# Attention keys placed by 64 KB SBUF-to-SBUF transfers instead of through DRAM

## The chip, the cores and the metric

The kernel runs on one core of a Trainium2 chip. The metric is the device time of one execution in microseconds; a kernel is given by the median of several runs. The profile is that of one execution.

## The reference

The input is x, [2048, 128] in float32. Four layers each do half a feed-forward, a mixer, and half a feed-forward again, each on the layer norm of x and added to x:

```python
x = x + 0.5 * _L2_ffn_ref(_layernorm(x, axis=-1), L2_ffn_w_gate, L2_ffn_w_up, L2_ffn_w_down)
x = x + _L2_attn_ref(_layernorm(x, axis=-1), L2_attn_Wq, L2_attn_bq, ...)
x = x + 0.5 * _L2_ffn_ref(...)
x = x + 0.5 * _L3_ffn_ref(_layernorm(x, axis=-1), L3_ffn_q_w, ...)
x = x + _L3_attn_ref(_layernorm(x, axis=-1), L3_attn_Wq, ...)
x = x + 0.5 * _L3_ffn_ref(...)
```

Layer 0 has a low-rank feed-forward and a causal attention of one head, layer 1 a mixture of 8 experts and a long convolution. The change is in layers 2 and 3, which hold four attentions of 16 heads with 8 dimensions a head:

```python
# L2 and L3 attention: rotary q and k (L3 is causal)
q, k = rope(x @ Wq + bq), rope(x @ Wk + bk)
ctx = softmax(q @ k.T / sqrt(8)) @ v          # per head
out = ctx @ Wo + bo
# each L3 feed-forward: attention with scaled scores, a gate, then experts
scores = q @ k.T / sqrt(8) * 2 * sigmoid(q . scale_w)
attn = (out * sigmoid(out @ gate_w + gate_b)) @ out_w
x = ln(src + attn); y = ln(x + the higher-numbered of the two best experts of x)
```

## The kernel before

x stays in SBUF. Its 2048 rows are worked in NC = 4 chunks of CW = 512. The four attentions run in the order rope2 (layer 2), gated[0] (layer 3's first feed-forward), rope3 (layer 3, causal) and gated[1] (layer 3's second feed-forward). There are 16 chunks of keys in all.

**Where keys live.** One SBUF tensor `kp` [128, 8, 2048] holds the keys of all heads: heads 2p and 2p+1 lie at free index p, in rows 0 to 63 and 64 to 127 (j is 0 or 1). In a half of 64 rows, the first 32 are four groups of 8 dimensions: high part, low part, high part, low part of the key. The query tile `qp` has high, low, low, high, so a single product of TensorE in a fast format gives all four partial products. `round_hi` (L747) makes the high part `hi`, a subtraction makes `lo`; both are [128, 512] tiles with one row for each head and dimension.

**How keys get there.** `send` (L688) writes `hi` and `lo` to a DRAM tensor `dk` (L694, two writes of 256 KB). `load_keys` (L707, transfers at L713) then reads them back in a different shape, 16 rows of `kp` for 4 values of p at a time: 8 transfers of 128 KB for a chunk, all on SP. Queries go the same way through `dq`, and `begin` (L865) loads those of a unit (one chunk of queries, four heads) with two `qp<-dq` transfers (L871).

**Order of work.** `attend` (L856) runs an attention. Its steps are interleaved with other work, and a mode says what may lie beside them: "free" outside `attend`, "fill" until the first weights are there, "core", and "drain", when all its own scores are made and the next attention's chunks are already prepared. In free and fill `queue()` (L608) alternates between ScalarE's and SP's queue; otherwise it is SP. `value` and `query` of the attention, `prepare` (L720: norm, keys, and for chunk 0 the query) of the next one, and the feed-forwards are generators that are advanced beside the loop. In free mode the key loads of a chunk wait in `waiting_keys` until `attend` begins, and it issues them before `begin`. In drain the first half (p 0 to 3) is loaded at once, the other half at the start of the next `attend`.

In core and drain, the order of TensorE and VectorE instructions is that of the program. Elsewhere a scheduler of the framework sets it, by readiness. Each engine works its own list in order, so a transfer's issue on ScalarE or SP that must wait holds everything behind it. Each transfer issued from SP or ScalarE uses one of 8 completion semaphores in turn, shared by the two queues, so that the nth waits until the (n-8)th has landed.

The rotary chunks take their tables `cos` and `sin` from DRAM (L763), on SP in free mode and on GpSimd's queue otherwise; `project` (L771) multiplies them on VectorE into `rot`, adds on GpSimd (L784), rounds to `hi` on ScalarE, and subtracts to `lo` on GpSimd (in drain: all on VectorE). `hi`, `lo`, `cos`, `sin`, `rot`, `xc`, `hid` and others share one ring of 10 tiles.

Key stages, and how each chunk of keys is made:

| stage | keys of | chunks made in free or fill | chunks made in drain |
| --- | --- | --- | --- |
| T1, 676 to 860 us | rope2 | 4 | 0 |
| T2, 1521 to 1665 us | gated[0] | 2 | 2 |
| T3, 2480 to 2640 us | rope3 | 4 | 0 |
| T4, 3100 to 3215 us | gated[1] | 1 | 3 |

Of the kernel before, what the change touches and what calls it, by code (L numbers as in the profile page):

```python
# [11 lines left out]
F32 = mybir.dt.float32  # L12
# [11 lines left out]
D = 128  # L24
NT = S // P
CW = 512
NC = S // CW
TC = CW // P
E = 8
NH = 16  # L30
HD = 8
# [3 lines left out]
KD = 64  # L35
# [7 lines left out]
def tile_macaron(ctx: ExitStack, tc: tile.TileContext, a: dict, out: bass.AP):  # L43
    nc = tc.nc
# [4 lines left out]
    dram = ctx.enter_context(tc.tile_pool(name="dram", bufs=1, space=DRAM))  # L49
# [18 lines left out]
    order = {"pinned": False, "mode": "free"}  # L68
# [23 lines left out]
    def transpose(dst, src):  # L92
# [8 lines left out]
        out=anti, in_=anti, compare_op=ALU.not_equal, fill=1.0, base=-(P - 1),  # L101
# [5 lines left out]
        out=mask_qk, in_=mask_qk, compare_op=ALU.is_ge, fill=NEG, base=0,  # L107
# [5 lines left out]
        out=mask_kq, in_=mask_kq, compare_op=ALU.is_ge, fill=NEG, base=0,  # L113
# [14 lines left out]
        out=before, in_=before, compare_op=ALU.is_ge, fill=1.0, base=0,  # L128
# [24 lines left out]
    for c in range(NC):  # L153
        loads[c % 2].dma_start(
            out=x[:, c * TC : (c + 1) * TC, :],
            in_=a["x"][c * CW : (c + 1) * CW, :].rearrange("(t p) d -> p t d", p=P),
# [451 lines left out]
    def queue():  # L608
        turn["q"] += 1
        return nc.scalar if order["mode"] in ("free", "fill") and turn["q"] % 2 else nc.sync  # L610
# [57 lines left out]
    class Heads:  # L668
# [19 lines left out]
        def send(self, which, c):  # L688
            hi, lo = ring("hi"), ring("lo")
            yield from self.project(which, c, hi.bitcast(F32R), lo.bitcast(F32R))  # L690
            parts = (hi, lo, lo, hi) if which == "q" else (hi, lo)
            d = (dq if which == "q" else dk)[c]
            for n, part in enumerate(parts):
                queue().dma_start(out=d[:, n * HD : (n + 1) * HD, :], in_=part)  # L694
            if which == "q":
                self.sent.add(c)
            elif self.current:
                self.load_keys(c)
            elif order["mode"] == "drain":
                self.load_keys(c, (0,))  # L700
                self.waiting_keys.append((c, (1,)))
            else:
                self.waiting_keys.append((c, (0, 1)))
            yield 1


        def load_keys(self, c, halves=(0, 1)):  # L707
            for h in halves:
                ps = slice(4 * h, 4 * h + 4)
                for j in range(2):  # L710
                    for n in range(2):
                        r = j * KD + n * 2 * HD
                        nc.sync.dma_start(  # L713
                            out=kp[r : r + 2 * HD, ps, c * CW : (c + 1) * CW].bitcast(F32),
                            in_=rows_of(dk[c], j)[:, ps, :],
                        )
            if 0 in halves:
                self.loaded.add(c)

        def prepare(self, c):  # L720
            yield from self.normed(c)
# [27 lines left out]
    def rows_of(d, j):  # L749
        return d.rearrange("(p j) r w -> j r p w", j=2)[j]  # L750

    class RopeHeads(Heads):
# [3 lines left out]
            self.v_weight = wp[pre + "_v"]  # L756
            self.xnT = {}

        def tables(self, c):
            for name in ("cos", "sin"):  # L760
                t = ring(name)
                where = nc.sync if order["mode"] == "free" else nc.gpsimd
                where.dma_start(out=t, in_=a[f"{self.pre}_{name}"][:, c * CW : (c + 1) * CW])  # L763
                yield t

        def normed(self, c):
# [2 lines left out]
            yield from normed_chunk(c, xn, self.xnT[c])  # L769

        def project(self, which, c, hi, lo):  # L771
            tables = list(self.tables(c))
            cols = self.wp[self.pre + "_bcol"]
            n = 0 if which == "q" else 2
            ps = banks("pj")
            for k, half in enumerate("AB"):
                mm(ps[:, k, :], self.wp[f"{self.pre}_{which}{half}"], self.xnT[c])
            turned = [ring("rot") for _ in range(2)]
            for k in range(2):
                vec.scalar_tensor_tensor(  # L780
                    turned[k], ps[:, k, :], cols[:, n + k : n + k + 1], tables[k], ALU.add, ALU.mult
                )
            engine = vec if order["mode"] == "drain" else nc.gpsimd
            engine.tensor_tensor(turned[0], turned[0], turned[1], ALU.add)  # L784
            round_hi(hi, turned[0])
            engine.tensor_tensor(lo, turned[0], hi.bitcast(F32), ALU.subtract)
            yield 1
# [68 lines left out]
    def attend(A, carried, follow, after=None):  # L856
# [1 line left out]
        KR = 4 * HD  # L858
        HV = HD + 1
        A.current = True  # L860
        for c, halves in A.waiting_keys:
            A.load_keys(c, halves)
        units, queries, weights = A.units, A.queries, A.weights

        def begin(B, u):  # L865
# [139 lines left out]
        n = nw = 0  # L1005
        while nw < len(weights) or last:
# [5 lines left out]
            if w and (ready.get(w[0], n + 1) > n or w[1] // TC not in A.valued):  # L1012
                w = None
# [380 lines left out]
    og = dram.tile([(E + XT) * P, D], F32, name="og")  # L1394

    rest = dram.tile([KD, CW], F32, name="rest")
    dk = [dram.tile([NH, 2 * HD, CW], F32, name=f"dk{c}") for c in range(NC)]
    dq = [dram.tile([NH, 4 * HD + 2, CW], F32, name=f"dq{c}") for c in range(NC)]
    def zero_tables():
        with tc.tile_pool(name="zero2", bufs=1) as tmp:  # L1400
# [80 lines left out]
def _rope_tables(ang):  # L1481
    half = HD // 2
    cos = np.empty((NH, HD, S), np.float32)
    sin = np.empty((NH, HD, S), np.float32)
    cos[:, :half], cos[:, half:] = np.cos(ang).T, np.cos(ang).T
    sin[:, :half], sin[:, half:] = -np.sin(ang).T, np.sin(ang).T
    return cos.reshape(D, S), sin.reshape(D, S)


def _layout(i):  # L1490
    f = np.float32
    half = HD // 2
# [12 lines left out]

    r = {
        "x": i["L0_attn_input_data"].reshape(S, D),
        "qk": i["L0_attn_qk"], "ov": i["L0_attn_ov"],
        "l0_WT": i["L0_ffn_W"].T, "l0_VT": i["L0_ffn_V_r"].T, "l0_CT": i["L0_ffn_C"].T,
        "l0_b": i["L0_ffn_b"],  # L1510
        "shift": shift,
        "aT": i["L1_attn_a"].reshape(NP, P).T,
        "bT": i["L1_attn_b"].reshape(NP, P).T,
        "cT": i["L1_attn_c"].reshape(NP, P).T,
        "l1_gT": i["L1_ffn_gate_w"].T,
        "l1_w12T": i["L1_ffn_w12"].transpose(2, 0, 1),
        "l1_w3T": i["L1_ffn_w3"].reshape(E, D, 2, P).transpose(3, 0, 2, 1),
        "l2_wgT": i["L2_ffn_w_gate"].T, "l2_wuT": i["L2_ffn_w_up"].T,
        "l2_wdT": i["L2_ffn_w_down"].reshape(D, 3, P).transpose(2, 1, 0),
    }  # L1520
    r["l2_cos"], r["l2_sin"] = _rope_tables(pos * inv2)
    r["l3_cos"], r["l3_sin"] = _rope_tables(pos * inv3)
    for pre, nm, t, oa, ob in (
        ("l2", "L2_attn", False, same, swap), ("l3", "L3_attn", True, odd_a, odd_b),
    ):
        w = {n: (i[f"{nm}_W{n}"].T if t else i[f"{nm}_W{n}"]) for n in "qkvo"}
        for n in "qk":
            r[f"{pre}_{n}A"], r[f"{pre}_{n}B"] = _ordered(w[n], oa), _ordered(w[n], ob)
        r[f"{pre}_bcol"] = np.stack(
            [_ordered(i[f"{nm}_b{n}"], o) for n in "qk" for o in (oa, ob)], axis=1,  # L1530
        )
        for n in "vo":
            r[f"{pre}_{n}"] = w[n]
            r[f"{pre}_b{n}"] = i[f"{nm}_b{n}"]

    sw = np.zeros((NH, HD, NH, HD), f)
    for h in range(NH):
        sw[h, :, h, :] = i["L3_ffn_scale_w"][h][:, None]
    r |= {
        "b3_q": i["L3_ffn_q_w"], "b3_k": i["L3_ffn_k_w"], "b3_sw": sw.reshape(D, D),  # L1540
        "b3_v": i["L3_ffn_v_w"], "b3_o": i["L3_ffn_out_w"], "b3_g": i["L3_ffn_gate_w"],
        "b3_gb": i["L3_ffn_gate_b"].reshape(D, 1),
        "b3_n1g": i["L3_ffn_n1_g"], "b3_n1b": i["L3_ffn_n1_b"],
        "b3_n2g": i["L3_ffn_n2_g"], "b3_n2b": i["L3_ffn_n2_b"],
        "b3_rs": i["L3_ffn_res_scale"],
        "b3_mg": i["L3_ffn_moe_gate_w"], "b3_mgb": i["L3_ffn_moe_gate_b"],
        "b3_b1": i["L3_ffn_b1"], "b3_b2": i["L3_ffn_b2"],
        "b3_wt": np.concatenate([
            i["L3_ffn_w1"],
            i["L3_ffn_w2"].reshape(E, 2, P, D).transpose(0, 2, 1, 3).reshape(E, P, 2 * D),  # L1550
            i["L3_ffn_ln_g"].reshape(E, 2, P).transpose(0, 2, 1),
            i["L3_ffn_ln_b"].reshape(E, 2, P).transpose(0, 2, 1),
        ], axis=2).reshape(E * P, WTN),
    }
    return {n: np.ascontiguousarray(v) for n, v in r.items()}
# [17 lines left out]
```

## Time and profile before

| what | value |
| --- | --- |
| median of 3 runs | 4069.42 us (4062.28 to 4075.64) |
| profiled execution | 4074.4 us, span 4072.6 us |
| TensorE busy | 3557.4 us (87%) |
| VectorE busy | 3141.5 us (77%) |
| ScalarE busy | 2329.1 us (57%) |
| GpSimd busy | 215.0 us (5%) |
| DMA | 111.91 MB, mean 27 GB/s |
| key loads `kp<-dk` | 128 of 128 KB |
| key writes `dk<-hi`, `dk<-lo` | 16 and 16 of 256 KB |

Times in the profile are microseconds from the start of the span. PE is TensorE, PEld its weight loads, DVE VectorE, ACT ScalarE, POOL GpSimd, SP the engine that issues most transfers; a q behind an engine's name (SPq, ACTq) means its issue of transfers. A group of instructions is written as "out<-in", with the line of the kernel. The number behind a bar, or in brackets, is the idle time of the engine just before the instruction, and "<-" names what ended it. The row of digits for the clock gives, for 40 equal slices, the TensorE clock that was granted, in tenths of full speed; the DMA row gives how busy the 16 DMA engines were.

### The profile page before, as it was taken

The numbers are of one execution on the slowest core, as the hardware profiler recorded it, in microseconds if no ns is written. First come the engines' busy times: TensorE is split into PE (matmuls) and PEld (weight loads), VectorE is DVE, ScalarE is ACT, GpSimd is POOL, SyncE is SP. The second block draws the span as 40 slices with busy tenths as digits, with TensorE's granted clock in tenths as the row PEclk, the third lists the DMA queues.
The fourth block names the chain that finished last, engine by engine and source line by source line (L and its number), as shares of the span: only waits on it lengthen the run. The fifth ranks groups of instructions, "written<-read, shape, count | busy, mean of one in ns | idle before, by whom it ended". The sixth has DMA issues, their size and how long they took to land. (4 is left out here: it accounts for less than half of the span.)

```text
span 4072.6 us, 72035 instructions
## 1 busy us (share of the span) xinstructions
PE 3557.4 (87%) x29080; PEld 1680.4 (41%) x29080; DVE 3141.5 (77%) x5645; ACT 2329.1 (57%) x4436; POOL 215.0 (5%) x262
## 2 busy tenths in 40 slices
PE   8789898689999995899999965599997899999965
PEld 8566664333333342333333343243333333333334
DVE  3855443579999975899999745689997799999844
ACT  1222122158888862688888722246675488888732
POOL 2000000100000000000000033100000000000013
PEclk8889798779999997899999966668998799999966
DMA  2100003220000002100000022400002200000012
GB/s 71 25 1 1 1 1 87 62 63 7 10 7 10 4 13 57 50 9 9 7 10 4 9 70 77 110 20 10 10 2 62 54 10 7 10 7 7 7 42 74
DMA packets 71532, 111.91 MB, mean 27 GB/s; under 512 B 9712, under 2 KB 29920, under 8 KB 70944
## 3 DMA queue, kind: packets, MB, share of 16 engines
q1 hardware_dynamic: 57536, 77.81, 7.2%
q0 software_dynamic: 7088, 20.81, 2.1%
q10 hardware_dynamic: 6576, 8.69, 0.8%
q8 instruction: 229, 3.75, 0.4%
q14 instruction: 103, 0.84, 0.1%
HBM read 74.47 MB, written 31.75 MB: 26 GB/s over the span
## 5 line engine op out<-in xcount | busy, mean ns | idle before, releaser
L83 DVE TENSOR_REDUCE h_mx<-sn 128x2 f32<-128x1024 f32 (+1 forms) x1856 | 2206.3, 1197 | 141.4 <-PE sn L886 119.8
L942 ACT ACTIVATE pr<-st 128x512 f32<-128x512 f32 x3712 | 1972.7, 585 | 518.7 <-PE st L75 335.7
L75 PE MATMUL av<-pr,va 128*32 128x256 f32 x14592 | 1191.4, 399 | 10.9 <-ACT h_ot L971 10.9
L75 PE MATMUL st<-qp,kp 64*128 64x512 f32 x3712 | 998.4, 500 | 49.2 <-ACT pr L942 45.6
L886 PE MATMUL sn<-kp,qp 64*128 64x512 f32 (+3 forms) x3712 | 812.1, 416 | 126.6 <-DMA qp<-dq 46.1
L75 PEld LDWEIGHTS st<-qp,kp 64*128 64x128 f32 x3712 | 394.4, 188 | 818.1 <-ACT pr L942 441.8
L75 PEld LDWEIGHTS av<-pr,va 128*32 128x32 f32 x14592 | 293.1, 109 | 664.7 <-issue 626.8
L886 PEld LDWEIGHTS sn<-kp,qp 64*128 64x128 f32 x3712 | 388.7, 195 | 186.6 <-issue 99.8
L75 PE MATMUL h<-xnT,w_l_w12T 128*128 128x512 f32 x512 | 250.1, 611 | 1.7 <-DVE xnT L65 1.7
L554 ACT ACTIVATE hid<-h 128x512 f32<-128x512 f32 x128 | 76.4, 597 | 301.4 <-PE h L75 301.4
L75 PEld LDWEIGHTS po<-w_l_w3T,hid 128*128 128x128 f32 x1024 | 131.2, 193 | 69.1 <-DVE hid L555 47.2
L563 DVE SCALAR_TENSOR_TENSOR x<-po,gate,x 128x128 f32<-128x128 f32 x256 | 71.9, 344 | 100.4 <-PE po L75 100.3
L75 PE MATMUL po<-w_l_w3T,hid 128*128 128x128 f32 x1024 | 139.9, 279 | 1.3 <-DVE hid L555 1.3
L555 DVE TENSOR_TENSOR hid<-hid,h 128x512 f32<-128x512 f32 x128 | 87.2, 683 | 55.1 <-PE h L75 55.1
L75 PEld LDWEIGHTS h<-xnT,w_l_w12T 128*128 128x128 f32 x512 | 90.2, 197 | 66.1 <-issue 62.6
L1270 POOL DMA_INDIRECT wt<-in_b_wt,w_row_i x30 | 28.8, 960 | 1436.6 <-DVE slot_i L83 1395.0
L915 ACT CAST h_mT<-mt_ps 8x512 fp32r<-8x512 f32 x64 | 36.9, 576 | 100.4 <-PE mt_ps L93 100.2
L83 DVE BATCH_NORM_STATS2 st<-ph 128x6 f32<-128x256 f32 x46 | 19.9, 432 | 87.0 <-PE ph L75 87.0
L223 POOL TENSOR_TENSOR x<-x,w_b_n2b 128x512 f32<-128x512 f32 x8 | 10.1, 1266 | 1301.1 <-DVE rows L83 1133.7
L93 PE MATMUL xn_tp<-ident,xn_t 128*128 128x128 f32 x64 | 20.1, 406 | 66.3 <-ACT xn_t L189 62.7
L83 DVE TENSOR_TENSOR sn<-sn,mask_qk 128x256 f32<-128x256 f32 x128 | 54.2, 426 | 30.7 <-PE sn L886 29.3
L83 DVE TENSOR_TENSOR st<-st,mask_kq 128x128 f32<-128x128 f32 x256 | 63.3, 291 | 14.0 <-PE st L75 13.4
(391 smaller groups left out, 2627.5 us busy)
## 6 DMA issues: line engine op xcount, KB each, us to landing
qp<-dq SPq DMA_DIRECT2D x128, 136.0 KB
kp<-dk SPq DMA_DIRECT2D x128, 128.0 KB
dq<-hi SPq DMA_DIRECT2D x23, 256.0 KB
dq<-lo SPq DMA_DIRECT2D x23, 256.0 KB
wt<-in_b_wt SPq DMA_DIRECT2D x16, 258.0 KB
kp<-rest SPq DMA_DIRECT2D x8, 512.0 KB
dk<-lo SPq DMA_DIRECT2D x16, 256.0 KB
qp<-h_mT SPq DMA_DIRECT2D x256, 4.0 KB
```

What stands on the lines that cost most here:

```text
L75: pin(nc.tensor.matmul(dst, lhsT=lhsT, rhs=rhs, start=start, stop=stop))
L83: ins = method(*args, **kw)
L93: pin(nc.tensor.transpose(dst, src, ident))
L223: nc.gpsimd.tensor_tensor(xs, xs, row.unsqueeze(1).to_broadcast([P, TC, D]), ALU.add)
L554: nc.scalar.activation(hid[:, hb, :], p_1, AF.Silu)
L555: nc.vector.tensor_tensor(hid[:, hb, :], hid[:, hb, :], p_2, ALU.mult)
L563: nc.vector.scalar_tensor_tensor(x[:, i, :], po[:, t, :], gate[:, i, e : e + 1], x[:, i, :], ALU.mult, ALU.add)
L886: pin(nc.tensor.matmul(sc[:, j, :wd], lhsT=qp[r, p, t * P : (t + 1) * P], rhs=kp[r, 2 * g + p, kc * CW : kc * CW + wd], start=True, stop=True,
L915: nc.scalar.copy(mT, pt)
L942: nc.scalar.activation(pr[:, off:CW], sc[:, off:], AF.Exp, scale=A.scale)
L1270: nc.gpsimd.indirect_dma_start(wts[k], None, a["b3_wt"], bass.IndirectOffsetOnAxis(ap=w_row_i[:, s - E : s - E + 1], axis=0),)
```

## The change

Keys made outside the drain go straight from `hi` and `lo` to `kp`, in 16 transfers of 64 KB a chunk: each takes 32 rows of `hi` or `lo` and fills 8 rows of `kp` for 4 values of p. They are issued from `queue()`, as soon as the chunk is made. In the drain, the first half goes this way (8 transfers on SP), the second is written to a smaller `dk` (two writes of 128 KB) and read back at the start of the next `attend` (8 transfers of 64 KB on SP).

For 32 neighbouring rows of `hi` to fill 8 rows for 4 values of p, the columns of the key weights, the key biases and the key tables are reordered when inputs are laid out (`by_rows`); for this, tables are now two sets, one for q and one for k, so the loads of the tables are as many as before. The issue order on SP also changes: without deferred loads, nothing of the keys stands at the start of `attend` except the second halves from the drain.

```diff
             if which == "q":
+                for n, part in enumerate(parts):
+                    queue().dma_start(out=dq[c][:, n * HD : (n + 1) * HD, :], in_=part)
                 self.sent.add(c)
-            elif self.current:
-                self.load_keys(c)
-            elif order["mode"] == "drain":
-                self.load_keys(c, (0,))
-                self.waiting_keys.append((c, (1,)))
+                yield 1
+                return
+            self.place_keys(c, 0, parts)
+            self.loaded.add(c)
+            if self.current or order["mode"] != "drain":
+                self.place_keys(c, 1, parts)
             else:
-                self.waiting_keys.append((c, (0, 1)))
+                for n, part in enumerate(parts):
+                    nc.sync.dma_start(out=dk[c][n], in_=part[KD:, :])
+                self.waiting_keys.append(c)
...
+        def place_keys(self, c, half, parts):
+            for n in range(4):
                 for j in range(2):
-                    for n in range(2):
-                        r = j * KD + n * 2 * HD
-                        nc.sync.dma_start(
-                            out=kp[r : r + 2 * HD, ps, c * CW : (c + 1) * CW].bitcast(F32),
-                            in_=rows_of(dk[c], j)[:, ps, :],
-                        )
+                    r, q = j * KD + n * HD, half * KD + j * 4 * HD
+                    queue().dma_start(
+                        out=kp[r : r + HD, 4 * half : 4 * half + 4, c * CW : (c + 1) * CW].bitcast(F32),
+                        in_=parts[n % 2][q : q + 4 * HD, :],
+                    )
+
+        def load_keys(self, c):
+            for n in range(4):
+                for j in range(2):
+                    r = j * KD + n * HD
+                    nc.sync.dma_start(
+                        out=kp[r : r + HD, 4:8, c * CW : (c + 1) * CW].bitcast(F32),
+                        in_=dk[c][n % 2].rearrange("(j d p) w -> j d p w", j=2, d=HD)[j],
+                    )
...
+    by_rows = np.arange(D).reshape(2, 4, 2, HD).transpose(0, 2, 3, 1).reshape(D)
...
+        for n in ("kA", "kB"):
+            r[f"{pre}_{n}"] = r[f"{pre}_{n}"][:, by_rows]
+        r[f"{pre}_bcol"][:, 2:4] = r[f"{pre}_bcol"][by_rows, 2:4]
...
-        "b3_q": i["L3_ffn_q_w"], "b3_k": i["L3_ffn_k_w"], "b3_sw": sw.reshape(D, D),
+        "b3_q": i["L3_ffn_q_w"], "b3_k": i["L3_ffn_k_w"][:, by_rows], "b3_sw": sw.reshape(D, D),
```

More of the change, by code (lines that the diff above doesn't have):

```diff
@@ L691, in send @@
             parts = (hi, lo, lo, hi) if which == "q" else (hi, lo)
-            d = (dq if which == "q" else dk)[c]
-            for n, part in enumerate(parts):
-                queue().dma_start(out=d[:, n * HD : (n + 1) * HD, :], in_=part)
             if which == "q":
+                for n, part in enumerate(parts):
+                    queue().dma_start(out=dq[c][:, n * HD : (n + 1) * HD, :], in_=part)
                 self.sent.add(c)
-            elif self.current:
-                self.load_keys(c)
-            elif order["mode"] == "drain":
-                self.load_keys(c, (0,))
-                self.waiting_keys.append((c, (1,)))
-            else:
-                self.waiting_keys.append((c, (0, 1)))
+                yield 1
@@ L704, in send @@
+                return
[3 more added lines that the diff above has]
+                self.place_keys(c, 1, parts)
+            else:
+                for n, part in enumerate(parts):
+                    nc.sync.dma_start(out=dk[c][n], in_=part[KD:, :])
+                self.waiting_keys.append(c)
             yield 1
-        def load_keys(self, c, halves=(0, 1)):
-            for h in halves:
-                ps = slice(4 * h, 4 * h + 4)
+        def place_keys(self, c, half, parts):
+            for n in range(4):
@@ L710, in load_keys @@
                 for j in range(2):
-                    for n in range(2):
-                        r = j * KD + n * 2 * HD
-                        nc.sync.dma_start(
-                            out=kp[r : r + 2 * HD, ps, c * CW : (c + 1) * CW].bitcast(F32),
-                            in_=rows_of(dk[c], j)[:, ps, :],
-                        )
-            if 0 in halves:
-                self.loaded.add(c)
+                    r, q = j * KD + n * HD, half * KD + j * 4 * HD
[3 more added lines that the diff above has]
+                    )
@@ L757, in __init__, with tables @@
             self.xnT = {}
-        def tables(self, c):
+        def tables(self, which, c):
             for name in ("cos", "sin"):
@@ L762, in tables @@
                 where = nc.sync if order["mode"] == "free" else nc.gpsimd
-                where.dma_start(out=t, in_=a[f"{self.pre}_{name}"][:, c * CW : (c + 1) * CW])
+                where.dma_start(out=t, in_=a[f"{self.pre}_{name}_{which}"][:, c * CW : (c + 1) * CW])
                 yield t
@@ L771, in project @@
         def project(self, which, c, hi, lo):
-            tables = list(self.tables(c))
+            tables = list(self.tables(which, c))
             cols = self.wp[self.pre + "_bcol"]
@@ L860, in attend @@
         A.current = True
-        for c, halves in A.waiting_keys:
-            A.load_keys(c, halves)
+        for c in A.waiting_keys:
+            A.load_keys(c)
         units, queries, weights = A.units, A.queries, A.weights
@@ L1396, in tile_macaron @@
     rest = dram.tile([KD, CW], F32, name="rest")
-    dk = [dram.tile([NH, 2 * HD, CW], F32, name=f"dk{c}") for c in range(NC)]
+    dk = [dram.tile([2, KD, CW], F32, name=f"dk{c}") for c in range(NC)]
     dq = [dram.tile([NH, 4 * HD + 2, CW], F32, name=f"dq{c}") for c in range(NC)]
@@ L1520, in _layout @@
     }
-    r["l2_cos"], r["l2_sin"] = _rope_tables(pos * inv2)
-    r["l3_cos"], r["l3_sin"] = _rope_tables(pos * inv3)
+    by_rows = np.arange(D).reshape(2, 4, 2, HD).transpose(0, 2, 3, 1).reshape(D)
+    for pre, inv in (("l2", inv2), ("l3", inv3)):
+        for n, t in zip(("cos", "sin"), _rope_tables(pos * inv)):
+            r[f"{pre}_{n}_q"], r[f"{pre}_{n}_k"] = t, t[by_rows]
     for pre, nm, t, oa, ob in (
```

## The prediction

> **What bounds the kernel now.** I read the page's totals first, then its slices, the costliest groups, the two DMA groups of the keys, and then the timeline of the four stretches in which keys are made.
>
> ```profile
> span 4072.6 us, 72035 instructions
> PE 3557.4 (87%) x29080; PEld 1680.4 (41%) x29080; DVE 3141.5 (77%) x5645; ACT 2329.1 (57%) x4436; POOL 215.0 (5%) x262
> PEclk8889798779999997899999966668998799999966
> DMA  2100003220000002100000022400002200000012
> L886 PE MATMUL sn<-kp,qp 64*128 64x512 f32 (+3 forms) x3712 | 812.1, 416 | 126.6 <-DMA qp<-dq 46.1
> kp<-dk SPq DMA_DIRECT2D x128, 128.0 KB
> ```
>
> TensorE is busy for 87%: inside an attention it sets the time, with VectorE close behind. No transfer of keys can matter there. It matters where the DMA row rises: these are the stages where keys are made, and the clock row dips at them (7 to 8, 6 in the third). Of the 126.6 us that TensorE was idle before `sn`, queries from DRAM ended 46.1. The busy time by stage:
>
> ```profile
> 676.00:860.00 184.00, 111.09 (x338) 53.55 (x336) 93.44 (x233) 30.73 (x61) 29.47 (x28) 0.69 0.41 103
> 860.00:1521.00 661.00, 653.29 (x6131) 253.76 (x6128) 622.93 (x679) 553.39 (x1027) 2.56 (x2) 0.99 0.02 7
> 1521.00:1665.00 144.00, 87.81 (x400) 41.81 (x398) 76.80 (x160) 35.64 (x68) 3.79 (x3) 0.75 0.28 67
> 2480.00:2640.00 160.00, 67.66 (x275) 33.62 (x276) 94.48 (x319) 34.29 (x78) 42.61 (x42) 0.63 0.39 102
> 3100.00:3215.00 115.00, 84.82 (x478) 38.27 (x477) 67.25 (x123) 44.15 (x87) 5.05 (x4) 0.74 0.37 86
> ```
>
> Columns: length, then busy time of TensorE, its weight loads, VectorE, ScalarE and GpSimd, the clock, DMA share, GB/s. In the four key stages T1 to T4 (603 us in all) no engine is full (TensorE 42 to 74%); the second row is an attention, where TensorE works 99%. So the end is set by a serial chain in T1 to T4: norm, projection, rotation, rounding, transfer, score. What queues on SP and ScalarE in these 603 us decides.
>
> **What the change removes and adds.** Before, each of 16 chunks of keys costs 2 writes of 256 KB and 8 loads of 128 KB: 10 transfers, 160 in all, the loads all on SP. After, the 11 chunks made outside the drain have 16 transfers of 64 KB (8 on ScalarE's queue, 8 on SP's); the 5 made in the drain (two in T2, three in T4) have 8, 2 writes of 128 KB, and 8 later loads, all on SP: 11 x 16 + 5 x 18 = 266. Compute is the same; tables for q and k are as many loads as before. What goes away is the DRAM round trip; what comes is 106 issues, and 8 x 11 = 88 key issues on ScalarE where `dk<-hi` was 11.
>
> **Price of one 64 KB transfer.** The trace has no such transfer, so I bound it. Issue: SBUF to SBUF exists in `qp<-h_mT`, four issues in 2.56 us, 0.64 us each. Eight on a queue are at least 8 x 0.64 = 5.1 us: the fast end. Flow:
>
> ```profile
> 1057.43 2.56 SPq L918 DMA_DIRECT2D qp<-h_mT  x4
> 670.00:690.00 20.00, 13.57 (x43) 7.24 (x42) 7.85 (x46) 5.46 (x12) 1.27 (x1) 0.76 1.07 206
> 819.00:824.00 5.00, 1.75 (x4) 0.78 (x4) 0.20 (x1) 0.00 (x0) 0.00 (x0) 0.50 1.07 155
> 1064.00:1068.00 4.00, 3.76 (x36) 1.64 (x32) 3.64 (x5) 3.12 (x7) 0.00 (x0) 1.00 0.15 55
> ```
>
> `kp<-rest` into 32 rows moves 206 GB/s, `kp<-dk` into 16 rows 155, and `qp<-dq` into 34 rows only 55, on 2 of 16 engines. [...] Each transfer also waits for the eighth before it on the two queues (8 completion semaphores in turn), which ties the queue that issues to landings.
>
> **T1, keys of rope2.**
>
> ```profile
> 697.40 0.60 SPq L694 DMA_DIRECT2D dk<-lo  x1
> 701.55 0.75 DVE L83 SCALAR_TENSOR_TENSOR rot<-pj,w_l_bcol,sin 128x512 f32<-128x512 f32 x1 [5.99 <-DMA sin<-in_l_sin]
> 729.50 0.53 ACTq L694 DMA_DIRECT2D dk<-hi  x1
> 731.39 0.60 ACT L646 ACTIVATE hid<-gu 128x512 f32<-128x512 f32 x1 [1.91 <-PE gu L75]
> 821.19 0.76 PE L886 MATMUL sn<-kp,qp 64*128 64x512 f32 x1 [12.88 <-DMA kp<-dk]
> ```
>
> Chunk 0: the q tables now stand on SP behind 8 key issues. VectorE already waits for `sin` (5.99 us), and behind it queue `xc` and the next chunk. Issues from 697.4 last 7 to 8 us, so 701.55 becomes about 708.5: +7 (fast +5, slow +16). Chunk 1: ScalarE issues its 8 from 729.5 until about 736.5 instead of 730.0; `hid`, due at 731.4, waits behind: +5 (fast +4, slow +11). Chunk 2 delays the `xc` copy in the same way, most of it covered by `hid`'s own chain: +1 (0.5 to 6). Chunk 3 is the direct path: lo is ready at 812.9, `sn` at 821.19, 8.3 us for write, receipt and first load, then 1 to 2 us more before 823.01. The new path needs about 6.5 for all pieces of half 0: -2 (fast -4, slow +2). Sum +11 (fast +5.5, slow +35).
>
> **T2, keys of gated[0].** In the drain SP alone carries 2 x 8 transfers and 4 writes ahead of q's four writes, so `qp<-dq`, which released `sn` at 1549.86, is about 3.5 later (0 to 8). Chunk 2 holds ScalarE ahead of `hid`: +1.5 (0 to 7.5). Chunk 3, with `sn` at 1642.24 after 4.63 us for `kp<-dk`: 0 (-2 to +6). Sum +5 (-1 to +21).
>
> **T3, keys of rope3: the gain.**
>
> ```profile
> 2551.80 0.53 SPq L694 DMA_DIRECT2D dk<-lo  x1
> 2552.37 15.29 SPq L713 DMA_DIRECT2D kp<-dk  x19
> 2568.21 11.34 SPq L871 DMA_DIRECT2D qp<-dq  x8
> 2573.51 0.44 PE L886 MATMUL sn<-kp,qp 64*128 64x128 f32 x1 [28.16 <-DMA qp<-dq]
> ```
>
> All key loads of three chunks are put off to the start of the attention and stand on SP ahead of the first query: TensorE idles 28.16 us. After, the keys are placed as they are made, and `qp<-dq` follows q's writes. Were nothing else late, `sn` could come about 21 us sooner. Against it: q's tables behind chunk 0's keys (+7), ScalarE's issues ahead of `xn_t` in chunks 0 and 1 (+3 to 4 each, one covered), and VectorE and TensorE work of the last experts that lay inside the idle 28 us must now be done after the first unit, some 5; the fourth chunk, made in the fill, holds ScalarE for +4. That is -21 + 7 + 4 + 5 + 4 = -1; since part of this lies in the same idle time (two holds at once count once), I take -4 (fast -14, slow +15).
>
> **T4, keys of gated[1].** As T2 with three drain chunks, but its chain has `sn` twice waiting for `qp<-dq` (11.29 and 1.88 us): +2 for the queue ahead of dq, +1 for 8-row loads of half 1, 0 for chunk 3: +3 (-2 to +17).
>
> **Sum.** 11 + 5 - 4 + 3 = +15 us. The profiled execution took 4074.4 with a span of 4072.6, so 4089.4 for such an execution. The runs of before have the median 4069.42 (4062.28 to 4075.64), 5.0 below the profiled one, so I put the +15 on the median: **4084 us**. All fast ends: 5.5 - 1 - 14 - 2 = -11.5; all slow ends: 35 + 21 + 15 + 17 = +88. Outside T1 to T4 I count nothing: TensorE covers it there (99% in the second row of stages). Were that cover gone, the 88 issues on ScalarE would cost 88 x 0.64 = 56 us; the part in T1 to T4 is priced above.
>
> **Rivals.** (A) The forecast. (B) Faster, by T3: if a chunk's transfers land in 5.1 us, the issue bound, the holds shrink to T1 +5.5, T2 0, T3 -16, T4 -1: -11.5 us, and -20 if the experts' work still fits into what idle time is left: 4050 to 4058. For it: 28.16 us of idle that only a queue's order causes, and 206 GB/s seen on one queue. Against: q's tables still stand behind 8 issues. It decides from about 5.5 us a chunk. (C) Costs and gain cancel: T3 gives -14 while T1, T2, T4 keep +14 to +19: 4068 to 4077. [...]
>
> **Chances.** About 0.3% (12 us) is what a measurement of this kernel can tell from no change. A 0.50, B 0.20, C 0.17, D 0.13. A's own range is 4072 to 4105, of which about a fifth lies within 0.3%. So faster 0.19 (B, nearly all beyond 4057), same 0.28 (C 0.17, a fifth of A, the edge of B), slower 0.53. The range for 8 in 10: leaving out the far end of D and of B, 4052 to 4122.
>
> **What would show it.** Right: in the page `kp<-hi` and `kp<-lo` on ScalarE's and SP's queues, 64 KB each; in T1 `rot` with `sin` near 708 and `hid` near 736, idle before them; in T3 the first `sn` well before 2573 with idle below 28.16; all of it within the key stages, the attentions unchanged in length. [...] Wrong: if the time moves inside the attentions, or the clock of T1 to T4 moves the sum.

## The result, and the profile after

The changed kernel takes 4115.93 us (median of 4 runs, 4104.34 to 4121.84), the kernel before on the same chip 4065.85 us (4051.9 to 4075.64). The ratio is 1.0122, with a 95% interval from 1.0083 to 1.0161: the change costs some 50 us. The forecast was 4084 us, with a range from 4052 to 4122.

The page of the changed kernel, the lines that answer to those of before:

```profile
span 4110.6 us, 72218 instructions
PE 3551.4 (86%) x29080; PEld 1671.1 (41%) x29080; DVE 3140.8 (76%) x5645; ACT 2327.7 (57%) x4436; POOL 215.1 (5%) x262
PEclk8999798679999997899999965578987799999966
L893 PE MATMUL sn<-kp,qp 64*128 64x512 f32 (+3 forms) x3712 | 811.1, 415 | 125.7 <-DVE h_mx L83 45.7
kp<-hi SPq DMA_DIRECT2D x64, 64.0 KB
```

Busy times are the same to 0.6%, so nothing is computed slower: TensorE waits longer. The 64 KB transfers are there (64 of each part on SP, 44 on ScalarE), and in the four slices around T3 (24th to 27th) the clock is 6, 5, 5, 7 where it was 6, 6, 6, 6. TensorE's idle time before `sn` is unchanged in sum (125.7 for 126.6), but `qp<-dq` no longer leads it. To see where the time went, I took the same instruction in both traces as a mark at each end of a key stage: T1 from the first cast `hi` of rope2 to its first `h_ot`; T2 from the 15th to the 17th `h_ot`; T3 from the first key projection of rope3 to the 41st `h_ot`; T4 from the 44th to the 49th `h_ot`. Before, these are 203.2, 226.6, 325.7 and 317.8 us (they are wider than the windows of the prediction). After:

| stage | forecast | measured |
| --- | --- | --- |
| T1 | +11 | +27.3 |
| T2 | +5 | +7.8 |
| T3 | -4 | +1.5 |
| T4 | +3 | +10.6 |
| sum | +15 | +47.2 |

Between the stages, the differences are under 1 us. The profiled spans differ by 38.0 and not 47.2 since this execution was 4.0 shorter ahead of T1 and 5.8 shorter behind T4, in work that the change doesn't touch.

T3's +1.5 is made of two parts of different kinds. Up to the first `h_ot` of rope3 it is 11.0 longer than before (119.0 for 108.0). From there to the end of T3 it is 9.4 shorter, and there the same 1346 products of TensorE take less time because the granted clock is 0.83 for 0.77. The two windows, before and after (columns as in the prediction; the clock is third from last):

```profile
2621.50:2839.10 217.60, 194.20 (x1346) 85.95 (x1346) 190.49 (x366) 113.37 (x246) 6.08 (x6) 0.77 0.08 25
2663.90:2872.10 208.20, 183.82 (x1346) 82.61 (x1346) 188.88 (x365) 112.66 (x246) 6.08 (x6) 0.83 0.08 26
```

So the placement of the keys lost 11 us in T3, and the clocks of these two executions hide 9.4 of it. (e7 below, which places keys as before, has the same 208.3 us and 0.83 in this part as the changed kernel.)

T1 and T3 in the changed kernel, from its timeline (VectorE and ScalarE in T1; TensorE and ScalarE in T3):

```profile
708.36 0.75 DVE L83 SCALAR_TENSOR_TENSOR rot<-pj,w_l_bcol,cos 128x512 f32<-128x512 f32 x1 [18.36 <-DMA cos<-in_l_cos_q]
749.75 1.08 ACT L646 ACTIVATE hid<-gu 128x512 f32<-128x512 f32 x2 [12.93 <-DMA kp<-hi]
2588.01 0.33 PE L893 MATMUL sn<-kp,qp 64*128 64x128 f32 x1
2597.28 1.26 ACT L189 ACTIVATE rows<-rows,ln_nb,ln_r 128x128 f32<-128x128 f32 x3 [12.44 <-DMA kp<-hi]
2612.09 1.02 PE L93 MATMUL mt_ps<-ident,h_mt 128*8 128x128 f32 x4
2624.24 1.65 ACT L189 ACTIVATE xn_t<-x,ln_nb,ln_r 128x128 f32<-128x128 f32 x4 [10.62 <-DMA kp<-hi]
2625.80 0.56 ACT L922 CAST h_mT<-mt_ps 8x512 fp32r<-8x512 f32 x1
2646.72 1.25 ACT L949 ACTIVATE pr<-st 128x384 f32<-128x384 f32 x3 [9.12 <-DMA kp<-hi]
```

VectorE stands 18.36 us for the q tables (before, 0.77 for `cos` and 5.99 for `sin`). ScalarE stands 12.93 us behind its own key issues before it can start `hid`. In T3 the first score comes without the 28.16 us of idle; counted from the start of the stage it is 17 us sooner. But between the scores and the exponentials (`pr`) stands a cast on ScalarE, `h_mT`, which the second product needs. Its input `mt_ps` is ready at 2613.1, and ScalarE comes to it at 2625.8, behind the issues of the third chunk's keys. Before, the first `h_mT` came 15.6 us after the first score; now it is 37.8. So the first exponential is 4.6 late. After the first four exponentials the issues of the fourth chunk take another 9.12 us, and the fifth is 10.8 late.

### The profile page after: what moved, and what is told of

Read it like the earlier page. It is cut to its first block, busy times and chain, and to the rows that moved or that the text cites. A ratio compares the mean times of both kernels' runs of the same rounds, so it can differ in the third digit from the quotient of the medians.

```text
span 4110.6 us, 72218 instructions
## 1 busy us (share of the span) xinstructions
PE 3551.4 (86%) x29080; PEld 1671.1 (41%) x29080; DVE 3140.8 (76%) x5645; ACT 2327.7 (57%) x4436; POOL 215.1 (5%) x262
## 5 line engine op out<-in xcount | busy, mean ns | idle before, releaser
L893 PE MATMUL sn<-kp,qp 64*128 64x512 f32 (+3 forms) x3712 | 811.1, 415 | 125.7 <-DVE h_mx L83 45.7
L75 PEld LDWEIGHTS po<-w_l_w3T,hid 128*128 128x128 f32 x1024 | 130.9, 192 | 68.8 <-DVE hid L555 47.2
L75 PE MATMUL gu<-xc,l_wgT 128*128 128x512 f32 x48 | 36.5, 852 | 45.7 <-DVE xc L65 23.5
```

Of the source, the lines that this page charges most:

```text
L75: pin(nc.tensor.matmul(dst, lhsT=lhsT, rhs=rhs, start=start, stop=stop))
L893: pin(nc.tensor.matmul(sc[:, j, :wd], lhsT=qp[r, p, t * P : (t + 1) * P], rhs=kp[r, 2 * g + p, kc * CW : kc * CW + wd], start=True, stop=True,
```

## The experiments

All stages are read as above, against the kernel before. Stages with the same code differed by 1.2 us in T1 (e8 and e9), 2.7 in T4 (e1, e9 and e11), 6 in T2 (e7 and before) and 8 in T3 (e4 and changed), so a stage's number from one profile is good to that. In T3 the 8 us lie behind its first `h_ot`: that last part took from 201.3 us (e4) to 217.7 (before), and over all kernels it is the longer the lower its clock, from 0.89 (e4) to 0.77 (before). The profile of before is the longest, so each T3 below is too low by 3 to 16 us. The column "T3, first" ends at the first `h_ot` and is nearly free of this; there changed and e4 differ by 1.2. Medians and ratios are of all runs, and they vary with the clock too: among the 31 runs of before beside e11, a mean clock lower by 0.001 goes with 2.3 us more (a line fitted to them).

| kernel | T1 | T2 | T3 | T3, first | T4 | sum of T1 to T4 | ratio to before (95%) |
| --- | --- | --- | --- | --- | --- | --- | --- |
| changed | +27.3 | +7.8 | +1.5 | +11.0 | +10.6 | +47.2 | 1.0122 (1.0083 to 1.0161) |
| e1 rows four apart | +10.8 | -1.0 | -8.9 | -5.4 | +5.7 | +6.6 | 1.0006 (0.9990 to 1.0022) |
| e2 q tables first | +17.7 | +6.9 | -8.1 | -2.1 | +10.3 | +26.8 | 1.0071 (1.0052 to 1.0091) |
| e3 keys on SP only | +22.1 | +8.3 | -13.2 | +0.7 | +13.3 | +30.5 | 1.0103 (1.0059 to 1.0147) |
| e4 drain undone, slowest dimension 4 | +27.4 | +12.7 | -6.7 | +9.8 | +10.3 | +43.7 | 1.0150 (1.0112 to 1.0189) |
| e5 rows two apart | +18.3 | +2.0 | -12.3 | -2.2 | +6.3 | +14.3 | 1.0026 (1.0015 to 1.0037) |
| e6 transfers of 128 KB | +24.3 | +26.9 | -5.5 | +3.9 | +30.9 | +76.6 | 1.0190 (1.0159 to 1.0222) |
| e7 before, query first | +0.4 | +5.8 | -10.8 | -1.4 | +0.4 | -4.2 | 0.9996 (0.9981 to 1.0010) |
| e8 e1, tables first, SP only | +0.2 | +8.4 | -21.6 | -12.2 | +12.7 | -0.3 | 1.0020 (1.0010 to 1.0031) |
| e9 as e8, both queues in fill | -1.0 | -2.0 | -7.4 | -1.2 | +3.4 | -7.0 | 0.9994 (0.9981 to 1.0008) |
| e10 e1 with 32 KB transfers | +31.0 | -0.4 | +4.2 | +9.5 | +20.7 | +55.5 | 1.0164 (1.0143 to 1.0185) |
| e11 e1 and tables first | +4.5 | -1.4 | -22.1 | -10.3 | +6.1 | -12.9 | 0.9981 (0.9969 to 0.9994) |
| e12 e5, tables first, drain undone | +7.6 | +0.3 | -19.0 | -9.6 | +0.0 | -11.1 | 0.9990 (0.9974 to 1.0006) |

The theory: a chunk's transfers take longer than the forecast had it, because 8 neighbouring rows of SBUF take data slowly (75 GB/s in chunk 0), and what stands behind them on SP and ScalarE waits that long. The rival: the number of issues is the price, whatever the flow.

**e1, rows four apart.** The rows of `kp` are interleaved, so that a transfer's 8 rows are four apart; q is written in the same order.

```diff
-                    r, q = j * KD + n * HD, half * KD + j * 4 * HD
+                    r, q = j * KD + n, half * KD + j * 4 * HD
                     queue().dma_start(
-                        out=kp[r : r + HD, ...
+                        out=kp[r : r + 4 * HD : 4, ...
...
-                    queue().dma_start(out=dq[c][:, n * HD : (n + 1) * HD, :], in_=part)
+                    queue().dma_start(out=dq[c][:, n : 4 * HD : 4, :], in_=part)
```

> The rows of a head group in kp are interleaved (row 4d+n instead of 8n+d), so each 64 KB transfer fills 8 rows that are 4 apart instead of 8 neighbouring ones; count, bytes, queues and waits are those of the changed kernel, and the result is the same. In the changed kernel a chunk's 16 transfers take 13.4 us in the first stage (78 GB/s), and the four key stages are longer than before by 27, 7.5, 2.5 and 10.7 us. [...] Rival 1 (the number of issues and their waits for the eighth before, not the flow): 13 us a chunk as now, 4116 us, ratio 1.012.

Measured: 4071.96 us, 44 less than the changed kernel with no transfer fewer. The windows of chunk 0's issues in T1, first the changed kernel (columns as in the prediction; GB/s last):

```profile
692.00:703.00 11.00, 0.00 (x0) 0.00 (x0) 0.00 (x0) 0.00 (x0) 1.26 (x1) 0.57 0.46 75
```

and with rows four apart:

```profile
691.60:698.60 7.00, 0.00 (x0) 0.00 (x0) 0.00 (x0) 0.01 (x1) 1.26 (x1) 0.62 0.33 118
```

11 us became 7, at 118 GB/s for 75. In the packet records of chunk 0 in the changed kernel, SP's first transfer runs at 0.08 us for 2 KB; SP's second and ScalarE's first take 0.16 to 0.17 in the mean, those behind them mostly 0.20 to 0.23, and the mean over the chunk is 0.19. With rows four apart it is 0.09. So it is the landing in neighbouring rows that backs up, and through the wait for the eighth transfer before it reaches the issues (SP waits 3.4 us for landings of keys in chunk 0, and for none in e1). The theory holds for chunk 0, where 11 us became 7. If the flow decides, the stages were expected at +11, +3, -12 and +5 against before: T1 and T4 came so, T2 4 better and T3 3 worse.

**e5, rows two apart**, the same edit with another stride.

```diff
-                    r, q = j * KD + n * HD, half * KD + j * 4 * HD
+                    r, q = j * KD + n // 2 * 2 * HD + n % 2, half * KD + j * 4 * HD
...
+                        out=kp[r : r + 2 * HD : 2, ...
```

> As the kernel with rows four apart, but two apart: 8 rows spread over 16 neighbouring ones. [...] Rival (only touching neighbours matter, any gap is enough): as with rows four apart, 0.09 us and 4068 to 4076 us.

Measured: 4081.0 us. The issues of chunk 0 took 7.1 us, as with rows four apart. Its packets took 0.10 us in the mean, for 0.09 in e1 and 0.19 in the changed kernel, so they back up a little. The rival was nearly right on the transfers, and wrong on the time. The window of these 7 us shows 117 GB/s, with transfers into both halves of `kp` under way at once, so what a single transfer into such rows moves isn't shown. Nor is it for 8 neighbouring rows: the 64 KB transfers alternate between the halves, and on SP alone (e3) the last of a chunk still followed one another at 0.75 us, 87 GB/s. The 7.5 us by which T1 is longer than in e1 are not from the transfers of chunk 0, and only 1 is from the issues of chunk 1 (ScalarE held 10.90 us for 9.82). From 676 to 900 us the clock was 0.66 for 0.73 in e1. Why is left open; over all runs the two kernels have the same median clock, 0.887, and e5 is still 0.2% slower.

**e2, q tables first.** For chunk 0, q's `cos` and `sin` are loaded before k's transfers.

```diff
-            tables = list(self.tables(which, c))
+            if which == "q" and c == 0:
+                tables = self.first
+            else:
+                tables = list(self.tables(which, c))
+            if which == "k" and c == 0:
+                self.first = list(self.tables("q", 0))
```

> The changed kernel, with the q tables of chunk 0 loaded ahead of its key transfers instead of behind them (one line moved in both rotary attentions). If the tables' place on SP is what delays the q rotation (708.4 instead of 694.8), it now comes with the k rotation, and the cast of q waits only until ScalarE has issued its 8 keys: some 9 us less in the first stage, up to 10 less in the third; 4097 to 4107 us. Rival (the q path is not the longest one there, the holds of ScalarE are): under 3 us in the first stage, 4110 to 4118 us.

Measured: 4097.26 us, at the near end. T1 is 9.6 shorter than in the changed kernel, and T3 9.6 too (13.1 up to its first `h_ot`). The rotation of q comes at once, and then its cast waits for ScalarE, as expected (timeline of this kernel):

```profile
694.67 0.75 DVE L83 SCALAR_TENSOR_TENSOR rot<-pj,w_l_bcol,cos 128x512 f32<-128x512 f32 x1 [0.97 <-DMA cos<-in_l_cos_q]
705.26 0.62 ACT L754 CAST hi<-rot 128x512 fp32r<-128x512 f32 x1 [9.58 <-DMA kp<-lo]
```

**e3, keys on SP only** (`queue()` in `place_keys` becomes `nc.sync`).

> The changed kernel, with all key transfers on SP, none on ScalarE. If ScalarE's holds (hid 11 us late in chunk 1, xc about 5 in chunk 2 of the first stage, 4 in the second, 9 in the third) cost on top of the tables: first stage 12 to 16 us shorter than in the changed kernel, second 3, third 3 to 6, fourth 0 to 2, so 4090 to 4098 us. If the flow alone decides (whoever waits, the keys come when they come): within 5 us of 4116. If one queue is slower than two: first scores later, over 4116.

Measured: 4113.49 us, so the second alternative, nearly no gain, though ScalarE holds nothing any more. In T1 only 5 us came back: the steps from k of chunk 1 to k of chunk 3 take together 92.4 us, 98.5 in the changed kernel, 82.1 before. In T2 and T4, where query loads follow on SP, it is 0.5 and 2.7 worse. The q of chunk 0 comes as late as in the changed kernel (19.3 us after k, 19.8 there), since 16 issues on one queue take 11.8 us, and tables and query loads stand behind them. T3 is 15 us shorter in this profile than in the changed kernel, 10.3 of it up to the first `h_ot` and 4.5 behind it at a clock of 0.87 for 0.83. The sum of the stages is 17 shorter, which the median does not show (2.4): the profile gives 7 back between the stages and 12 ahead of T1 and behind T4.

**e6, transfers of 128 KB.** Outside the drain, 8 transfers for all 8 p, still into 8 neighbouring rows; the drain goes through DRAM.

```diff
+                    r, q = j * KD + n * HD, j * KD
                     queue().dma_start(
+                        out=kp[r : r + HD, :, c * CW : (c + 1) * CW].bitcast(F32),
+                        in_=parts[n % 2][q : q + KD, :],
```

> Outside the drain 8 transfers of 128 KB a chunk instead of 16 of 64 KB (columns ordered so that 64 neighbouring rows of hi or lo fill 8 neighbouring rows of kp for all 8 p); the drain goes through DRAM as before. It is compared with the kernel that has the free part alone (first stage +27 against before, second +13, third -7, fourth +10). [...] If the flow alone sets the time of what waits: packets 0.19 to 0.21 us, the first stage +24 to +27. If the flow works through the wait for the eighth transfer before: ScalarE is free after 4 issues, about 3 us, hid in chunk 1 is not held 13 us, and the first stage comes to about +12 to +16, the third to -12. If the number of issues is all: first stage about +8.

Measured: 4149.88 us; T1 +24.3, the first alternative by its number, though not flow alone: with 4 issues for 8, `hid` in chunk 1 still stands 9.09 us behind ScalarE's issues (12.93 in the changed kernel). The timeline of this kernel, SP and VectorE:

```profile
702.64 0.33 SPq L770 DMA_DIRECT2D cos<-in_l_cos_q  x1
713.60 0.75 DVE L83 SCALAR_TENSOR_TENSOR rot<-pj,w_l_bcol,cos 128x512 f32<-128x512 f32 x1 [19.32 <-DMA cos<-in_l_cos_q]
```

SP's issues of chunk 0 are over after 3.6 us, yet q's tables, issued at 702.64, are used at 713.60. In the packet records the tables follow SP's keys, which end at 705.1, and their first packets take 0.36 us in the mean while ScalarE's keys still land, until 712.2; the last take 0.09. So the tables wait for the backed-up keys without any issue in between. T2 and T4 (+27, +31) are my experiment's fault. In its layout, the slowest dimension of the drain's DRAM writes is 2, and the window of these writes shows little of the DMA engines in use:

```profile
1547.00:1559.00 12.00, 10.65 (x84) 3.91 (x76) 5.05 (x14) 9.91 (x19) 0.00 (x0) 1.00 0.13 44
```

44 GB/s and a DMA share of 0.13, as much as two of sixteen engines. From the first of these writes to the first load behind them it is 13.4 us; before, with a slowest dimension of 16, 3.7 us. T2 and T4 of e6 therefore say nothing about the size of the transfers.

**e10, 32 KB transfers** with rows four apart: each transfer outside the drain split in two halves of its columns, so 32 a chunk instead of 16.

> [...] It prices the issues where the flow no longer binds (packets 0.09 us). If the issues are then what holds: a chunk's issues take 13 to 14 us instead of 7, the first stage grows by 12 to 18 us (from +10.8), time 4095 to 4110 us. If what is left is latency of the last transfer: within 5 us of 4072.

Measured: 4132.59 us, 61 more than e1. T1 grew by 20, T3 by 13, T4 by 15, and the time lies beyond the 4095 to 4110 expected. In its chunk 1 ScalarE issues 16 from 738.61 to 752.77 and `hid` waits:

```profile
752.82 1.09 ACT L646 ACTIVATE hid<-gu 128x512 f32<-128x512 f32 x2 [14.24 <-DMA kp<-hi]
```

Here nothing backs up (1 KB packets at 0.046 us). So the rival is true as well, beside the theory: an issue costs 0.67 us on SP and 0.68 on ScalarE, plus its wait, and once 16 of them a chunk are cheap to land, their number is the rest of the price. Chunk 0 held its queues for 11 us with the flow into neighbouring rows, 7 us with 16 issues, 12.5 us with 32.

**e4, the drain undone**, all else as changed.

> The changed kernel, with the chunks made in the drain sent through DRAM again as before (two writes of 256 KB, 128 KB loads); the 11 others by the 64 KB transfers. By stages the drain part lies in the second (two chunks) and fourth (three chunks), which are 7.5 and 10.7 us longer than before: expected to come back to about +4 and +3, so 4104 to 4108 us, and stages one and three as in the changed kernel (+27, +2.5). Rival (the drain part is hidden by the weights of the attention before): no difference, 4113 to 4118 us.

Measured: 4131.12 us, no gain, rather a loss. It did not test what it was to: to undo the drain with the new column order, the writes to `dk` got a slowest dimension of 4, and from the first write to the first load it is 9.1 us, before the change, with 16, 3.7. T3, with the same code as changed, came 8 us lower, at a clock of 0.89 for 0.83 behind its first `h_ot`. The profiled execution was the fastest of four (4116.85), so its stages show less of the loss than the median.

**e12, the drain undone with another layout** (`dk` as [32, 2, 4, 512], so that a write has 32 as its slowest dimension), on the ground of e5 with tables first.

> [...] Its drain issues are then 2 writes and 8 loads of 128 KB a chunk, as before the change. If the drain's 18 issues cost what the second and fourth stages lost (with rows two or four apart +2 or -1, and +6 each time): second about 0, fourth 0 to +2, first +4, third -20, so 4050 to 4058 us, ratio 0.9955 to 0.9985. If the fourth stage stays at +6: the loss there is in the chunk made in the fill, and the time is that of the kernel with rows four apart and tables first, 4059.

Measured: 4058.44 us, with T2 +0.3 and T4 +0.0. From the first write of the drain to the first load it is 3.2 us in T4, before the change 3.6. The first alternative for T4: its +6 with rows two or four apart comes from the drain's 18 transfers on SP (10 here), though their number and their kind are not told apart. The ratio, 0.9990, is just above the range expected. T3 up to its first `h_ot` is that of e11 within 1. T1 is 3 longer, more than the spread of T1; rows two apart made it longer in e5 too, and this stays open.

**e7, the query first, in the kernel before.** Nothing of the change but the order at the start of `attend`.

```diff
-        for c, halves in A.waiting_keys:
-            A.load_keys(c, halves)
...
+        first = units[0] not in queries
+        for c, halves in A.waiting_keys:
+            A.load_keys(c, halves)
+            if first:
+                begin(A, units[0])
+            first = False
```

> The kernel before with one thing moved: at the start of an attention the first unit's query is loaded after the keys of chunk 0, not after those of all waiting chunks. It isolates the gain that the change was to have in the third stage, where TensorE is idle 28.2 us before the first score. If that wait is on the path: first score some 12 to 18 us sooner, but work of the last experts follows it, so the stage 5 to 12 us shorter, 4055 to 4062 us. If the idle time only covers later keys: stage within 3 us, 4064 to 4070 us. Stages one, two and four as before.

Measured: 4072.34 us, ratio 0.9996, for the 4055 to 4062 of the first alternative. T3 is 10.8 shorter, as that had it, but not for its reason. The first score comes 9.4 sooner and the first exponential 4.8, yet the first `h_ot` only 1.4. The other 9.4 lie behind it, where the clock is 0.83 for 0.77. So the second alternative holds: asking for the query sooner gains next to nothing. What takes its place between the first score and the first `h_ot` isn't taken apart. In the profile T2 is 5.8 longer, though its instructions stand in the same order there. From 1600 to 1612 us the kernel before, and then e7:

```profile
1600.00:1612.00 12.00, 7.44 (x29) 4.60 (x28) 4.91 (x6) 2.37 (x4) 0.00 (x0) 0.76 0.56 89
```

```profile
1600.00:1612.00 12.00, 8.86 (x27) 5.58 (x26) 3.73 (x4) 1.77 (x3) 0.00 (x0) 0.50 0.57 89
```

The granted clock is 0.50 for 0.76: products take longer, the same work stretches. Whether it does so in most runs isn't shown; with it the sum of the stages is -4.2, within what the ratio allows (0.9981 to 1.0010).

**e8, e9 and e11: the parts together.** e8 is rows four apart, tables first and all keys on SP; e9 the same with both queues in the fill; e11 both queues everywhere.

> The changed kernel with rows four apart, q tables ahead of the keys, and all key transfers on SP. The stages of the kernel with rows four apart are +10.8, -1.0, -8.9, +5.7 against before. Without ScalarE's holds and the tables' wait the first stage should come to 0 to +4, the third to -14 to -20, the second and fourth stay: -10 to -16 in all, 4051 to 4057 us, ratio 0.996 to 0.9975. Rival (16 issues on one queue, 10.7 us at the least, become the wait): sum near +5, 4070 us.

> The changed kernel with rows four apart, q tables ahead of the keys, and key transfers on SP alone in free mode but on both queues in the fill. With all of them on SP the stages were +0.2, +8.4, -21.6, +12.7; with both queues (rows four apart) the second and fourth were -1.0 and +5.7. If the queues of the fill make the difference: 0, 0, -20, +6, sum -14, 4052 to 4060 us, ratio 0.995 to 0.9985. Rival (stages two and four vary by the granted clock, not by the queue): +8 and +12 again, ratio 1.000 to 1.003.

> The changed kernel with rows four apart and q tables ahead of the keys, key transfers on both queues as in the changed kernel. The tables gave 9.6 us in both the first and third stage with neighbouring rows; with rows four apart q waits less (issues end after 7 us, ScalarE's at 6.5): first stage 2 to 5 us under +10.8, third 3 to 8 under -8.9, second and fourth as with rows four apart (-1, +6): 4058 to 4066 us. If the tables gain nothing more: 4072.

Measured: 4080.22, 4066.05 and 4059.35 us. In e8 T1 is even with before and T3 21.6 shorter (12.2 up to its first `h_ot`), but with 16 issues ahead of the query loads in the fill T2 and T4 lose as much, and the median is 8 us above before. In e9 these come back (-2.0, +3.4), as expected, and T3 loses 14 of its gain, 11 of them up to its first `h_ot`: before its first exponential ScalarE stands behind the keys of the fourth chunk (timeline of e9):

```profile
2589.04 1.28 ACT L955 ACT_TABLE_LOAD   x1 [7.31 <-DMA kp<-hi]
```

e11, where the expectation was 4058 to 4066, is the fastest: ratio 0.9981, 0.9969 to 0.9994, so it beats both kernels, by 8 us and by 57. The 57 are beyond doubt. The 8 are clear of the interval, but no stage accounts for them. In T3 its first score, at 2554.22, is 16 us sooner than before, counted from the start of the stage, and its first `h_ot` 10.3:

```profile
2554.22 0.33 PE L898 MATMUL sn<-kp,qp 64*128 64x128 f32 x2
```

The rest of its -22.1 is the clock behind it, 0.86 for 0.77. With T1 +4.5, T2 -1.4 and T4 +6.1 the placement comes to about -1, and the median clock of its runs is 0.890 for 0.887 in those of before. Whether that clock comes from the change isn't shown.

## Why the prediction was right in direction and too small

**The place and the mechanism of the cost were right; T3 was not.** The placement moved the time in T1 to T4, and the attentions between them kept their length to under 1 us. The q tables behind chunk 0's keys, `hid` behind ScalarE's issues, the queries behind the drain, and the earlier first score of rope3 all show as described. The sign is right. That 4116 lies in the range is due to its width: three of the four terms were too small, and T3, which was to pay for a part, cost 11 us. The text named a moving clock in T1 to T4 as a sign of being wrong: it moved the profile's T3 by 9.4, and so the sum.

**The term that was mis-sized is the price of a chunk.** The forecast lets a chunk's issues last 7 to 8 us in T1. That was the author's estimate, and no run shows it for neighbouring rows: there chunk 0 took 11 us at 75 GB/s. Issue alone would be 7 (e1). Nor does a run show the slow ends of T1, +16 and +11 for chunks 0 and 1, or the 6.5 us for half 0 of chunk 3: these steps came to +11.5, +12.3 and -0.5. The 206 GB/s that B calls on have a DMA share of 1.07, all 16 engines. The 64 KB transfers of chunk 0 had 0.46, and with rows four apart the same transfers moved 118 GB/s at 0.33. (T2's fast end adds up to -2, not -1, and with it the fast ends to -12.5.) In T1, by the casts of k and q in both traces:

| step of T1 | before | after | difference | forecast |
| --- | --- | --- | --- | --- |
| k of chunk 0 to q | 8.3 | 19.8 | +11.5 | +7 |
| q to k of chunk 1 | 25.1 | 25.0 | 0 | 0 |
| k of chunk 1 to k of chunk 2 | 24.1 | 36.4 | +12.3 | +5 |
| to k of chunk 3 | 58.0 | 62.1 | +4.1 | +1 |
| to the first `h_ot` | 87.7 | 87.2 | -0.5 | -2 |

**Chunk 1 was mis-sized by a second thing**: the wait for the eighth transfer before counts all transfers, and here four are slow query loads: SP's issue at 747.74 starts when the query load eight before it has landed, at 747.73. The waits of SP from 736 to 752 us in the changed kernel (total, times, longest):

```profile
SPq L713 <- DMA qp<-dq: 8.1, 2, 7.1
```

The text named this tie, and priced it at nothing. With rows four apart chunk 1's issues still take 11.2 us, not 7, and in the changed kernel ScalarE's packets of chunk 1 take only 0.08 to 0.11 us in the mean of each transfer: here the waits hold, and not the landing. Of the +12.3 in that step, rows four apart save 3.4.

**T3 was to gain and lost.** The gain of 21 less the tables' 7 came as 17 at the first score. The step that failed is what stands against it. The text had 13 us there: +4 for ScalarE's issues in chunks 0 and 1, +5 for the last experts' work, +4 for the fill. Measured, 28 us went between the first score and the first `h_ot`. ScalarE stood 12.44 us before the experts' `rows`, 10.62 before `xn_t` with `h_mT` behind it, and 9.12 in the fill. So that part is +11.0, for -4. e7 shows how little the idle 28.16 us were worth: with the query first and nothing else changed, the first score came 9.4 sooner and the first `h_ot` 1.4. That the whole stage reads +1.5 is the clock behind the first `h_ot`, as told under the result.

**T2 and T4.** +7.8 for +5 and +10.6 for +3. In T4 the drain's transfers on SP were worth 6 (e12), where the text had +2, and +1 for 8-row loads, which no run shows on its own; the rest is the flow, 5 (e1). In T2, e1 removes all.

**The rivals.** D is the case in which the landing of the transfers, and not their issue, sets the wait. That is what chunk 0 shows, at 75 GB/s and 0.19 us a packet, for 0.09 with rows four apart. The speed that D took for the landing is shown by no run. B's condition, about 5.5 us a chunk, was not met in any kernel: 8 issues on each of two queues are 7 us with their gaps. Its place was right: with cheap landings and early tables T3 gains 10.3 up to its first `h_ot` (e11), not the 16 to 21 that B had.

## What to carry to other kernels

Leaving out a round trip through DRAM saved nothing here, since the many small transfers that took its place were issued by queues on which the serial chain also stands: count the issues, at 0.67 us here, and ask what is queued behind each. An idle engine before a step is a gain only if nothing else is due by the next step: follow the chain to the first thing that it delivers (in e7 a first score 9.4 us sooner gave 1.4 at the first `h_ot`). Give a transfer into few SBUF rows rows that are apart, not neighbours: that alone was worth 44 us here, with the same transfers and bytes. Put the loads that the next step waits for ahead of a bulk placement (9.6 us of T1 in e2). Check the slowest dimension of every transfer that an edit reshapes: with 2 for 16 it was 13.4 us from the drain's first write to its first load, for 3.7 (e6).

## What the runs showed beyond what I had expected

Transfers into 8 neighbouring rows start at 0.08 us for a 2 KB packet and slow down only as more follow: on two queues from each one's second on, to 0.20 to 0.23 in the mean; on SP alone from the eighth or so on, to 0.20 at the end of the chunk (e3). A single one measured alone would look free. A gap of one row was enough for 0.10 at 117 GB/s (e5). A stage whose instructions stand in the same order moved by 5.8 us with a granted clock of 0.50 for 0.76 over 12 us of it (e7), and the end of T3 by up to 16 us, with clocks from 0.77 to 0.89. So a gain of this size in one stage of one profile must be read up to a mark before which the clock has done nothing, or set beside the busy time of the same products.
